# Second-layer expert biases added through the tokens' gates, transfers counted by the instruction scheduler, and eight sequences routed as 4 + 4 instead of 2 + 3 + 3

## The chip, the cores and the metric

The kernel runs on one core of a Trainium2 chip. The metric is the device time of one execution in microseconds (us). Matrix products run on TensorE (PE in the profile, its weight loads PEld), elementwise work on VectorE (DVE), ScalarE (ACT) and GpSimd (POOL). SyncE (SP) issues most of the transfers, and POOL issues the ones that gather or scatter rows by an index.

## The reference

Two layers act on eight sequences of 512 tokens with 128 channels. In each layer an attention and an expert layer read the same normalized input, and both are added to it.

```python
xn = layernorm(x)
x  = x + L0_attn(xn, ...) + L0_ffn(xn, ...)     # linear attention; top-1 of 8 experts, 128 -> 128
xn = layernorm(x)
x  = x + L1_attn(xn, ...) + L1_ffn(xn, ...)     # windowed + latent attention; top-2 of 8 experts

# L1_ffn
probs  = softmax(x_flat @ gate_w.T)
topk_probs, topk_idx = top_k(probs, 2)
hidden = relu(einsum('th,ehf->tef', x_flat, w1) + b1)        # 128 -> 512
all_out = einsum('tef,efh->teh', hidden, w2) + b2            # 512 -> 128
y = sum over the two chosen experts of all_out * topk_probs
```

In layer 1 a token's output from an expert is multiplied by the token's gate, so the part that comes from `b2` is the token's two gates times the two rows of `b2`.

## The kernel before

**Stages.** `layer0(b)` runs the first layer of sequence b: norm, projections, linear attention, and eight products with the expert weights, each with the tokens scaled by a gate (`gbc`, a gate row read back from DRAM and spread over the partitions). It ends with the normalized tokens written to `x_rows[h]` and router logits kept for group h. `attention1(b)` is the second layer's attention. Its last steps are `loc` (DVE), `aT` (POOL; the tile `aT` has one buffer), the product `fp` of `aT` with `wo1`, and an addition of `fp` to the sequence's `x1`.

**Groups.** `GROUPS` splits the sequences for the second expert layer. `route(h)` needs the logits of all sequences of group h. It finds the two best experts of each token (`pick`), their gates (`gw`), and sorts tokens by expert into tiles of 128 rows; each expert's rows are rounded up to whole tiles. It ends with `token_i` and `row_i`, the indices to gather by and to scatter to. `experts1(h)` then runs over a fixed number of tiles, `_tiles(n) = (2 * n * N + E * (P - 1)) // P` for n sequences: 23, 31 and 31. For a tile it loads w1 and w2 of the tile's expert (256 KB each) and its row of b2 spread over the partitions (64 KB), all through SP with an expert number read on the chip. POOL gathers 128 rows (`xgt`), PE transposes them (`tpx`), multiplies by w1 (`hp`), ACT adds b1 and applies the relu (`ht`), PE multiplies by w2 (`yp`), DVE adds b2 (`ys`) and POOL scatters the rows to `y_rows`. `output(b)` waits for all scatters of the group, reads two rows per token back (`yg`), multiplies them by the gates and adds them to `x1`.

**Order.** No engine chooses its order while running. The stages are first written down by a `Recorder` (line 127). `_duration` (line 395) gives each instruction a planned time and a delay after which others may use its result, `PLAN` (line 1461) gives each stage a start and an end that are turned into a rank for each instruction, and `order()` (line 238) picks, again and again, the instruction that can begin first by the planned times, and of several the one with the lower rank. Engines then execute in that order: a waiting instruction holds back all that are behind it on its engine. A DMA is planned here as the issuing engine's time and a fixed delay; what other transfers are doing does not enter. `_fill` (line 349) puts products of zeros (from line 362) ahead of a PE instruction where the plan sees a pause of 0.6 us or more and the output bank allows it.

In profile rows, buffer and sequence numbers are left out of the names. Nearly all instructions carry the line of the recorder's call, L389, so rows are told apart by tile names.

Of the kernel before, what the change touches and what calls it, by code (L numbers as in the profile page):

```python
# [10 lines left out]
F32 = mybir.dt.float32  # L11
# [3 lines left out]
ALU = mybir.AluOpType  # L15
# [4 lines left out]
P = 128  # L20
B, N, C = 8, 512, 128
H, D = 16, 8
NT = N // P
# [7 lines left out]
CHUNK = N // NLAT  # L31


GROUPS = (2, 3, 3)
GROUP_OF = [(h, i) for h, n in enumerate(GROUPS) for i in range(n)]


# [79 lines left out]
class Op:  # L117
# [1 line left out]

    __slots__ = (  # L120
        "engine", "emit", "uses", "time", "delay", "rank", "after", "before", "start", "end",
        "missing", "opens", "claims", "index", "follows", "shape", "last", "room",
    )


class Recorder:
# [6 lines left out]
    AHEAD, TURN = 60.0, 0.15  # L133

    PAUSE, FILL = 0.6, 0.8
    filled = 0
    ENGINES = {"tensor": "PE", "vector": "DVE", "scalar": "ACT", "gpsimd": "POOL", "sync": "SP"}

# [18 lines left out]
        yield  # L157
        self.group, self.share = None, 1.0

    def add(self, engine, emit, writes, reads, time, delay, shape=None):  # L160
        uses = [(a, True) for a in writes] + [(a, False) for a in reads]
        time *= self.share
        if engine == "PE" and self.ops and self.ops[-1].engine == "PE":

            op = self.ops[-1]
            same = op.uses[0][0].tensor.name == writes[0].tensor.name
            if self.group == len(self.ops) - 1 or (self.group is None and same):
                op.emit.append(emit)
                op.uses += uses
                op.time += time + (self.TURN if shape != op.last and self.group is None else 0.0)  # L170
                op.last = shape
                return
        op = Op()
        op.engine, op.emit, op.time, op.delay = engine, [emit], time, delay
        op.shape = op.last = shape
        op.index, op.follows = len(self.ops), ()
        op.uses = uses
        self.ops.append(op)
# [59 lines left out]
    def order(self):  # L238
# [24 lines left out]
        by_rank = sorted(self.ops, key=lambda op: (op.rank, op.index))  # L263
        oldest = 0
        free = dict.fromkeys(("PE", "DVE", "ACT", "POOL", "SP"), 0.0)
        shape = None
        ready = {e: [] for e in free}
        for op in self.ops:
# [5 lines left out]
        while len(out) < len(self.ops):  # L274
# [45 lines left out]
            op.room = at - max([free[e]] + [promised[t.name] for t in op.opens])  # L320
            op.start, op.end = at, at + turn + op.time
            free[e] = op.end
            for t in uses.get(op.index, ()):
                left[t.name] -= 1
                holders[t.name] = max(holders.get(t.name, 0.0), op.end + op.delay)
                if not left[t.name]:
                    slots[t.tag].append(holders[t.name])
            for other in op.before:
                lag = op.delay
                if other.engine == e and lag < 1.0:  # L330
                    lag = 0.0 if e == "PE" else 0.05
                other.start = max(other.start, op.end + lag)
                other.missing -= 1
                if not other.missing:
                    ready[other.engine].append(other)
# [33 lines left out]
class _Engine:  # L369
# [3 lines left out]
    def __getattr__(self, method):  # L373
        r, name = self._r, self._name
        call = getattr(getattr(r.nc, name), method)

        def record(*args, **kwargs):
            aps = [a for a in (*args, *kwargs.values()) if isinstance(a, bass.AP)]
            aps += [
                a.ap for a in (*args, *kwargs.values()) if isinstance(a, bass.IndirectOffsetOnAxis)  # L380
            ]
            time, delay = _duration(name, method, aps)
            shape = None
            if name == "tensor":
                rows = aps[1].shape[0]
                cols = int(np.prod(list(aps[1].shape)[1:])) if method == "matmul" else P
                shape = (rows, 32 * ((cols + 31) // 32))
            r.add(
                r.ENGINES[name], lambda: call(*args, **kwargs), aps[:1], aps[1:], time, delay, shape  # L389
            )  # L390

        return record


def _duration(engine, method, aps):


    def free(ap):
        return int(np.prod(list(ap.shape)[1:]))

    out = free(aps[0])
    if "dma" in method:
        size = 4e-6 * int(np.prod(list(aps[0].shape)))
        return (1.25, 2.4) if engine == "gpsimd" else (0.5, 2.0 + 5.0 * size)
    if engine == "tensor":
        if method == "transpose":
            return 0.13, 0.2
        if "16" in str(aps[2].tensor.dtype):
            return max(0.0006 * free(aps[2]), 0.04), 0.2
        return 2 * max(0.00094 * free(aps[2]), 0.064 + 0.00047 * free(aps[1])), 0.2  # L410
    n = max([out] + [free(a) for a in aps[1:2]])
    if engine == "scalar":
        if method == "copy":
            return (0.18 if aps[0].shape[0] == 32 else 0.08) + 0.00084 * n, 0.16
        return 0.26 + 0.0011 * n if len(aps) == 4 else 0.17 + 0.00095 * n, 0.16
    if engine == "gpsimd":
        if method == "memset":
            return 0.08 + 0.0005 * n, 0.08
        if n < 8:
            return 1.05, 0.08  # L420
        alike = int(np.prod([c for step, c in list(aps[2].ap)[1:] if step]))
        return 0.05 + (0.002 if alike <= 16 else 0.0024) * n, 0.08
    if method == "reciprocal":
        return 0.09 + 0.0062 * n, 0.12
    sbuf = all("PSUM" not in str(a.space) for a in aps)
    fast = sbuf and method in ("tensor_scalar", "tensor_scalar_mul", "tensor_scalar_add", "tensor_copy", "memset")
    both = sbuf and n < 1024 and len(aps) > 2 and free(aps[2]) > 1
    return (
        0.095 + (0.28 if len(aps) == 4 and (n == P or n < 8) else 0.0)
        + (0.0009 if fast else 0.0016 if both else 0.00102) * n,  # L430
        0.12,
    )
# [3 lines left out]
def two_layers_kernel(  # L436
# [67 lines left out]
    load(wsb[:, w_first:], wpack[:, w_first:])  # L504
    we_sb = const.tile([P, E, C], F32, name="we_sb")
    load(we_sb, expert_w, nc.scalar)

    ro_sb = const.tile([P, C], F32, name="ro_sb")
    for half in (slice(0, LC), slice(LC, P)):
# [204 lines left out]
    for h, n in enumerate(GROUPS):  # L714
# [1 line left out]
        rows = 2 * max(GROUPS) * N + _tiles(n) * P  # L716
        y_rows.append(tc.nc.dram_tensor(f"y_rows_{h}", [rows, C], F32, kind="Internal").ap())
        logits.append(keep.tile([P, n * NT, E], F32, tag=f"logits{h}", name=f"logits_{h}", bufs=1))
    places = {}


    OTHER = {
# [200 lines left out]
    def attention1(b):  # L923
# [216 lines left out]
        nc.vector.scalar_tensor_tensor(loc, gsb[:, 0, :], 1.0, pv, ALU.add, ALU.mult)  # L1140
        nc.gpsimd.tensor_tensor(aT, aT, loc, ALU.add)
        yield
        fp = bank("fp" + nm)
        for t in range(NT):
            ts = slice(t * P, (t + 1) * P)
            mm(fp[:, ts], aT[:, ts], wo1)
        xf = x1.rearrange("p t c -> p (t c)")
        nc.vector.tensor_add(xf, xf, fp)
        late[b] = x1
# [2 lines left out]
    def route(h):  # L1152
# [17 lines left out]
        nc.vector.tensor_tensor(gw[:, 1], mx2, mx, ALU.subtract)  # L1170
        nc.scalar.activation(gw[:, 1], gw[:, 1], AF.Exp, bias=zero)
        nc.vector.tensor_mul(gw[:, 1], gw[:, 1], rs)
        m = small.tile([P, GT, E], F32, tag="ex16", name="m" + nm, bufs=1)
        nc.vector.tensor_add(m, pick[:, 0], pick[:, 1])
        mf = m.rearrange("p t e -> p (t e)")
# [133 lines left out]
    def experts1(h):  # L1309
# [6 lines left out]
        def fetch(j):  # L1316
# [12 lines left out]
                fetch.last = nc.ops[-1]  # L1329
            first = work.tile([P, FF], F32, tag="w1", name=f"w1{nm}_{j}", bufs=3)  # L1330
            second = work.tile([P, NFC, C], F32, tag="w2", name=f"w2{nm}_{j}", bufs=4)
            third = work.tile([P, C], F32, tag="b2", name=f"b2{nm}_{j}", bufs=4)

            def load_first():
                e = bass.ds(numbers[j // QUAD][j % QUAD], 1)
# [3 lines left out]
                e = bass.ds(numbers[j // QUAD][j % QUAD], 1)  # L1339
                tc.nc.sync.dma_start(second, w2[e].rearrange("e (k p) c -> p (e k) c", p=P))  # L1340

            def load_third():
                e = bass.ds(numbers[j // QUAD][j % QUAD], 1)
                tc.nc.sync.dma_start(third, experts_b[e, 1].to_broadcast([P, C]))

            for move, to in ((load_first, first), (load_second, second), (load_third, third)):
                nc.add("SP", move, [to], [], 0.55, 3.3)
                nc.ops[-1].follows = (fetch.last,)
            ws[j] = first, second, third

        def gather(q):
            js = range(q * QUAD, min((q + 1) * QUAD, TILES))
# [13 lines left out]
        def scatter(j, ys):  # L1366
# [5 lines left out]
                    views[j], bass.IndirectOffsetOnAxis(ap=ids, axis=0), ys, None  # L1372
                )

            nc.add("POOL", store, [], [ys, ids], 1.25, 2.4)
            scattered[h].append(nc.ops[-1])

        def turn(q):
# [18 lines left out]
        for j in range(TILES + 1):  # L1397
# [18 lines left out]
                hts[j] = ht  # L1416
                yield
            if j:
                ht, (_, w2k, b2) = hts.pop(j - 1), ws.pop(j - 1)
                yp = bank(f"yp{nm}_{j - 1}")  # L1420
                for k in range(NFC):
                    mm(
# [1 line left out]
                        start=k == 0, stop=k == NFC - 1,  # L1424
                    )
                ys = work.tile([P, C], F32, tag="ys", name=f"ys{nm}_{j - 1}", bufs=YS)
                nc.vector.tensor_add(ys, yp[:, :C], b2)
                scatter(j - 1, ys)
                yield

# [21 lines left out]
    def load_next(b):  # L1452
        xs[b] = load_x(b)
        if b == 1:
# [6 lines left out]
    PLAN = {  # L1461
        "load": ((0, 1), (46, 47), (92, 93), (138, 139), (184, 185), (230, 231), (276, 277)),
        "layer0": (
            (0, 1), (0, 10), (1, 39), (77, 134),
            (121, 154), (178, 309), (241, 418), (313, 760),
        ),
        "route": ((68, 100), (273, 384), (789, 901)),
        "attention1": (
            (33, 150), (148, 194), (204, 270), (284, 611),
            (549, 789), (924, 1084), (1023, 1271), (1198, 1498),  # L1470
        ),
        "experts1": ((68, 410), (427, 1006), (967, 1293)),
        "output": (
            (676, 701), (627, 663), (1181, 1203), (995, 1107),
            (1262, 1379), (1408, 1425), (1456, 1524), (2493, 2506),
        ),
    }

# [77 lines left out]
```

## Time and profile before

| | |
|---|---|
| time, median of 3 runs (lowest to highest) | 643.65 us (640.91 to 647.41) |
| the profiled execution, own time | 641.01 us |
| its span, first to last instruction | 639.1 us |
| mean granted TensorE clock | 0.947 |
| PE busy / DVE busy / POOL busy / ACT busy | 563.8 / 476.3 / 402.7 / 343.9 us |
| moved by DMA | 91.63 MB, mean 143 GB/s |

Busy times are unions: where two instructions of one engine overlap, the overlap counts once. In a row for a group of instructions, the busy time is that of the group and the mean is the duration of one instruction. An fp32 matrix product shows as two matmul instructions, a transpose as one. So 85 tiles with four products each give 680 instructions `hp`.

### The profile page before, as it was taken

To read this page: it belongs to the slowest core of one execution; us is meant where nothing else is said; L and a number is where in the kernel's file an instruction comes from. 1 tells how busy PE (TensorE), PEld (TensorE's weight loads), DVE (VectorE), ACT (ScalarE), POOL (GpSimd) and SP (SyncE) were. 2 spreads that over 40 slices of the span, in tenths; PEclk is the share of its full clock that TensorE was granted. 3 is DMA by queue.
4 is the path that set the end of the run, shared out by engine and by line. 5 is a ranking of instruction groups with operands and counts; after the bars stand their busy time and mean duration, and the time that the engine had idled before them with its cause. 6 is when DMAs were issued, how large, how long until landed. Compare 5 with 4: busy or idle time off the path is not lost.

```text
span 639.1 us, 15660 instructions
## 1 busy us (share of the span) xinstructions
PE 563.8 (88%) x5487; PEld 465.2 (73%) x5487; DVE 476.3 (75%) x1297; ACT 343.9 (54%) x950; POOL 402.7 (63%) x422
## 2 busy tenths in 40 slices
PE   9989888798899898789999799888798988999894
PEld 3478576487777687678978679878586777888852
DVE  2797899979898899997768777878437552856594
ACT  3624639354947754475774474543744347457620
POOL 3045143788678559647668768867668586787562
PEclk8999999899999999999979899798989799899986
DMA  4044135264434246247545665677457485687222
GB/s 153 19 145 137 66 102 147 53 187 123 126 98 120 64 158 148 58 140 213 150 129 164 185 188 179 155 216 211 156 179 196 129 237 141 171 238 245 60 83 67
DMA packets 106532, 91.63 MB, mean 143 GB/s; under 512 B 8940, under 2 KB 84086, under 8 KB 106454
## 3 DMA queue, kind: packets, MB, share of 16 engines
q1 hardware_dynamic: 100582, 78.41, 42.1%
q0 software_dynamic: 5440, 11.15, 6.3%
q10 hardware_dynamic: 432, 1.07, 0.5%
q8 instruction: 44, 0.72, 0.5%
q14 instruction: 34, 0.28, 0.1%
HBM read 80.70 MB, written 9.90 MB: 142 GB/s over the span
## 4 chain that ended last, share of the span: by engine, by line
PE 37%; DVE 28%; POOL 12%; issue 9%; ACT 6%; DMA 6%; SPq 0%; POOLq 0%; DVEq 0%; ACTq 0%
PE yp L389 7%; PE hp L389 6%; PE sc L389 4%; DMA gbc<-gd 3%; POOL m L389 3%; PE rp L389 3%; DVE pw L389 3%; PE pv L389 3%; DVE xg L389 2%; POOL pw L389 2%; POOL xgt L389 2%; POOL y_rows L1371 2%; DVE m L389 2%; POOL xg L389 2%; DVE x L389 2%
## 5 line engine op out<-in xcount | busy, mean ns | idle before, releaser
L389 ACT ACTIVATE ht<-hp,bias 128x128 f32<-128x128 f32 x340 | 101.4, 373 | 51.2 <-PE hp L389 34.1
L1371 POOL DMA_INDIRECT y_rows<-ys,row_i x85 | 88.1, 1036 | 48.4 <-issue 9.8
L389 POOL DMA_INDIRECT xgt<-x_rows,token_i x85 | 87.4, 1029 | 24.8 <-issue 18.6
L389 PE MATMUL yp<-w,ht 128*128 128x128 f32 x680 | 94.6, 286 | 1.9 <-issue 1.6
L389 PEld LDWEIGHTS hp<-xt,w 128*128 128x128 f32 x680 | 86.6, 198 | 12.7 <-issue 6.7
L389 PE MATMUL hp<-xt,w 128*128 128x128 f32 x680 | 94.4, 285 | 1.2 <-DVE ys L389 0.7
L389 PEld LDWEIGHTS yp<-w,ht 128*128 128x128 f32 x680 | 86.9, 199 | 7.3 <-issue 5.3
L389 PE MATMUL rp<-we_sb,xg 128*128 128x128 f32 x512 | 67.9, 281 | 6.3 <-POOL xg L389 4.7
L389 PEld LDWEIGHTS rp<-we_sb,xg 128*128 128x128 f32 x512 | 62.2, 194 | 11.9 <-POOL xg L389 7.4
L389 POOL TENSOR_TENSOR xg<-xT,gbc 128x512 f32<-128x512 f32 x32 | 42.8, 1338 | 37.3 <-DMA gbc<-gd 25.9
L389 PE MATMUL pv<-pw,vb 128*32 128x64 f32 (+1 forms) x1088 | 37.9, 226 | 15.6 <-POOL pw L389 11.5
L389 PE MATMUL sc<-kT,qe 32*128 32x64 f32 x1024 | 45.7, 296 | 6.1 <-issue 4.8
L389 PEld LDWEIGHTS pv<-pw,vb 128*32 128x32 f32 x1088 | 33.7, 117 | 23.5 <-POOL pw L389 16.5
L389 PEld LDWEIGHTS sc<-kT,qe 32*128 32x128 f32 x1024 | 40.2, 205 | 11.9 <-issue 7.5
L389 POOL TENSOR_TENSOR pw<-pt,csb 128x512 f32<-128x512 f32 x32 | 42.5, 1328 | 3.5 <-DVE pt L389 3.3
L389 POOL TENSOR_TENSOR m<-m,amx 128x512 f32<-128x512 f32 x32 | 33.8, 1065 | 14.7 <-DVE amx L389 12.8
L389 POOL TENSOR_TENSOR m<-m,ard 128x512 f32<-128x512 f32 x32 | 34.4, 1076 | 12.7 <-DVE ard L389 3.4
L389 DVE TENSOR_TENSOR ys<-yp,b 128x128 f32<-128x128 f32 x85 | 23.5, 278 | 23.6 <-PE yp L389 19.5
L389 DVE TENSOR_TENSOR pw<-pt,csb 128x512 f32<-128x512 f32 x32 | 40.6, 1268 | 0.3
L389 POOL TENSOR_TENSOR le<-le,lrd 128x128 f32<-128x128 f32 (+3 forms) x32 | 24.0, 756 | 25.3 <-DVE lrd L389 18.3
L389 DVE COPY_PREDICATED m<-csb,sc 128x256 f32<-128x256 int32 x64 | 25.3, 435 | 19.5 <-issue 7.9
L389 ACT ACTIVATE m<-m,zero_b 128x512 f32<-128x512 f32 x32 | 23.2, 724 | 29.6 <-POOL m L389 29.6
(261 smaller groups left out, 1232.6 us busy)
## 6 DMA issues: line engine op xcount, KB each, us to landing
w<-in_w_dram SPq DMA_DIRECT2D x170, 256.0 KB
gbc<-gd SPq DMA_DIRECT2D x64, 256.0 KB
b<-in_experts_b_dram SPq DMA_DIRECT2D x85, 64.0 KB
yg<-y_rows SPq DMA_DIRECT2D x16, 256.0 KB
x<-in_x_dram SPq DMA_DIRECT2D x8, 256.0 KB
x_rows<-xn SPq DMA_DIRECT2D x8, 256.0 KB
out_dram<-x SPq DMA_DIRECT2D x8, 256.0 KB
xgt<-x_rows,token_i POOLq DMA_INDIRECT x85
```

The lines of the kernel that those rows point to most:

```text
L389: r.ENGINES[name], lambda: call(*args, **kwargs), aps[:1], aps[1:], time, delay, shape
L1371: tc.nc.gpsimd.indirect_dma_start(views[j], bass.IndirectOffsetOnAxis(ap=ids, axis=0), ys, None)
```

## The change

Three things change together, and the two tables that go with them.

- The groups are 4 and 4 sequences. `_tiles` then gives 39 and 39 tiles, 78 in place of 85.
- b2 is no longer loaded per tile and added to each tile's rows. It is loaded once, 8 rows of 128. `route` sums the two gated one-hot choices to `gates` (tokens by experts, two DVE instructions); `attention1(b)` transposes them (four PE transposes and an ACT copy, in `gate_rows`) and multiplies them with `b2_sb` into the bank `fp`, ahead of the products of `aT`. The move of `yp` out of PSUM, `ys`, becomes a copy on ACT.
- The recorder gives DMAs a `traffic`, the planned time for which they occupy the transfer engines. Transfers are queued one behind another in the plan, and a transfer's result is there no earlier than its traffic and `LANDING` allow. A few planned durations change (POOL's DMA delay, small DVE instructions).
- `PLAN` has other numbers for the two-group order.

```diff
-GROUPS = (2, 3, 3)
+GROUPS = (4, 4)
...
+    LANDING = 1.5
...
+            op.lag = op.delay
+            if op.traffic:
+                carried = max(carried, op.end) + op.traffic
+                op.lag = max(op.lag, carried + self.LANDING - op.end)
...
-                lag = op.delay
+                lag = op.lag
...
+            traffic = 0.0
+            if "dma" in method:
+
+                rate = 2.6 if len(aps[0].shape) == 2 and aps[0].shape[1] >= 512 else 3.3
+                traffic = rate * 4e-6 * int(np.prod(list(aps[0].shape)))
...
-        return (1.25, 2.4) if engine == "gpsimd" else (0.5, 2.0 + 5.0 * size)
+        return (1.25, 3.0) if engine == "gpsimd" else (0.5, 2.0 + 5.0 * size)
...
+    b2_sb = const.tile([E, C], F32, name="b2_sb")
+    load(b2_sb, experts_b[:, 1])
...
+        h, hb = GROUP_OF[b]
+        gT = gate_rows(gates1[h][:, hb * NT : (hb + 1) * NT], "1" + nm, lambda pool, sh, tag, name: (
+            work.tile(sh, F32, tag="loc", name=name, bufs=1)
+        ))
         fp = bank("fp" + nm)
-        for t in range(NT):
-            ts = slice(t * P, (t + 1) * P)
-            mm(fp[:, ts], aT[:, ts], wo1)
+        tiles = [slice(t * P, (t + 1) * P) for t in range(NT)]
+        for ts in tiles:
+            mm(fp[:, ts], gT[:, ts], b2_sb, start=ts.start == 0, stop=False)
+        for ts in tiles:
+            mm(fp[:, ts], aT[:, ts], wo1, start=False, stop=ts.stop == N)
...
+        both = small.tile(sh, F32, tag="rpw", name="gated" + nm, bufs=1)
+        nc.vector.tensor_tensor(both, pick, gw.unsqueeze(3).to_broadcast(sh), ALU.mult)
+        gates = small.tile([P, GT, E], F32, tag="gates", name="gates" + nm)
+        nc.vector.tensor_add(gates, both[:, 0], both[:, 1])
+        gates1[h] = gates
...
-            third = work.tile([P, C], F32, tag="b2", name=f"b2{nm}_{j}", bufs=4)
...
-            def load_third():
-                e = bass.ds(numbers[j // QUAD][j % QUAD], 1)
-                tc.nc.sync.dma_start(third, experts_b[e, 1].to_broadcast([P, C]))
-
-            for move, to in ((load_first, first), (load_second, second), (load_third, third)):
-                nc.add("SP", move, [to], [], 0.55, 3.3)
+            for move, to, traffic in ((load_first, first, 0.67), (load_second, second, 0.86)):
+                nc.add("SP", move, [to], [], 0.55, 3.3, traffic=traffic)
...
-                nc.vector.tensor_add(ys, yp[:, :C], b2)
+                nc.scalar.copy(ys, yp[:, :C])
...
         "layer0": (
-            (0, 1), (0, 10), (1, 39), (77, 134),
-            (121, 154), (178, 309), (241, 418), (313, 760),
+            (0, 13), (0, 24), (16, 86), (63, 165),
+            (136, 273), (251, 319), (306, 378), (334, 412),
         ),
-        "route": ((68, 100), (273, 384), (789, 901)),
+        "route": ((135, 253), (395, 497)),
         "attention1": (
-            (33, 150), (148, 194), (204, 270), (284, 611),
-            (549, 789), (924, 1084), (1023, 1271), (1198, 1498),
+            (16, 154), (125, 174), (255, 299), (325, 379),
+            (370, 528), (509, 643), (725, 946), (869, 1072),
         ),
-        "experts1": ((68, 410), (427, 1006), (967, 1293)),
+        "experts1": ((291, 469), (503, 868)),
```

## The prediction

> **What bounds the kernel now.** I read the page's busy times first, then the costliest groups, then asked the trace for where the expert tiles and the routing indices begin and end, and last for busy times in stretches cut at those points.
>
> ```profile
> PE 563.8 (88%) x5487; PEld 465.2 (73%) x5487; DVE 476.3 (75%) x1297; ACT 343.9 (54%) x950; POOL 402.7 (63%) x422
> ...
> L389 PE MATMUL yp<-w,ht 128*128 128x128 f32 x680 | 94.6, 286 | 1.9 <-issue 1.6 <-ACT ht L389 0.3
> L389 PE MATMUL hp<-xt,w 128*128 128x128 f32 x680 | 94.4, 285 | 1.2 <-DVE ys L389 0.7 <-ACT gsb L389 0.2 <-issue 0.2
> ...
> L389 DVE TENSOR_TENSOR ys<-yp,b 128x128 f32<-128x128 f32 x85 | 23.5, 278 | 23.6 <-PE yp L389 19.5 <-PE tpx L389 1.4 <-PE hp L389 1.2
> ...
> L389 PE MATMUL fp<-wo,aT 128*128 128x128 f32 x64 | 9.5, 295 | 4.7 <-POOL aT L389 4.7
> L389 PE MATMUL gp<-csb,g 128*8 128x128 f32 x32 | 5.6, 288 | 1.7 <-issue 0.8 <-ACT gsb L389 0.5 <-DVE g L389 0.4
> ```
>
> PE is the fullest engine. The mean of one `hp` is 285 ns, but 94.4 / 680 is 139 ns: products are pipelined, so I price PE work by a group's busy time over its count. A tile is 1.11 (`hp`) + 1.11 (`yp`) + 0.17 (`tpx`, 14.4 us over 85) = 2.4 us of PE.
>
> ```profile
> L389 PE MATMUL hp<-xt,w x680: 272/275/583, 130.1 to 598.7; 128*128 128x128 f32 x170
> L389 PE MATMUL yp<-w,ht x680: 270/275/582, 133.4 to 601.3; 128*128 128x128 f32 x170
> L389 DVE SCALAR_TENSOR_TENSOR row_i<-row,none x3: 182/192/192, 114.4 to 450.0; 128x31 int32<-128x31 f32 x2, 128x23 int32<-128x23 f32 x1
> ```
>
> These rows of tiles give first and last start. The first routing is done at 114.4 us, the first tile's product starts at 130.1, the last tile's at 601.3, and 37 us follow. Busy time by stretch (columns: stretch, length, then PE, PEld, DVE, ACT, POOL busy, granted PE clock, DMA share, GB/s):
>
> ```profile
> 0.00:114.00 114.00, 102.03 (x674) 71.92 (x675) 89.23 (x299) 59.24 (x142) 36.50 (x56) 0.99 0.36 110
> 114.00:130.00 16.00, 12.06 (x113) 6.72 (x112) 12.61 (x40) 6.08 (x11) 11.51 (x12) 0.80 0.15 35
> 130.00:214.00 84.00, 76.09 (x843) 64.36 (x842) 72.02 (x192) 52.65 (x137) 65.74 (x64) 1.00 0.43 126
> 214.00:330.00 116.00, 105.56 (x1037) 90.40 (x1035) 101.33 (x303) 70.96 (x194) 74.19 (x75) 0.98 0.51 143
> 330.00:480.00 150.00, 133.09 (x1383) 118.68 (x1381) 103.65 (x250) 81.03 (x245) 110.59 (x115) 0.93 0.60 176
> 480.00:601.00 121.00, 109.51 (x1175) 96.41 (x1175) 71.19 (x162) 68.82 (x212) 86.05 (x87) 0.94 0.65 183
> 601.00:640.00 39.00, 25.47 (x271) 16.68 (x270) 26.26 (x57) 5.09 (x11) 18.10 (x16) 0.77 0.25 72
> ```
>
> Three regimes. Up to 130 us there are no expert tiles and DVE sets the pace; PE's busy time there includes products of zeros. From 130 to 601 PE is about 90% busy in every stretch, whatever DVE does. The end is one attention's dependency chain with PE mostly idle or on zeros.
>
> **Work removed and added.** Removed with 7 of 85 tiles: PE 7 x 2.4 = 16.8 us, POOL 14 gathers and scatters of 1.03 us (14.4 us), ACT 28 `ht` of 0.30 us (8.4). Removed with the b2 loads: 85 `ys` additions, 23.5 us of DVE. Of transfers, 85 x 64 KB and 7 tiles' weights and rows, about 10 of 91.6 MB, and 99 issues on SP. Added: on PE 32 gate transposes (as `gp`, 5.6 us) and 64 instructions for gates times `b2_sb`. These use 8 of 128 rows, but the trace shows no discount for that: `we` from a one-row operand took 632 ns an instruction against 619 for one of 128 rows. So as `fp`, 9.5 us. PE's real work goes from 16.8 down to 15.1 up: nothing gained. ACT gains 78 copies, priced at the 268 ns of a 128x128 copy `pT` (21 us), and 8 of 0.57: +17 net on an engine 54% busy. It takes the place of DVE behind `yp`, for one-third of a microsecond either way; I put it at nothing, with ACT's idle time as cover (-3 to +5 us). DVE falls by about 21 us, but where PE or a chain is the bound that is worth little.
>
> So the gain has to come from placement, and I take the two instruction orders engine by engine. For every instruction ahead of a point I add its row's busy time over count. Such sums exceed the page's busy time, since neighbours overlap: over the whole program PE 661 against 563.8 (0.853) and DVE 546 against 476.3.
>
> **Step 1: the first tile comes later.** Ahead of the first `row_i` DVE has, before, 105 us of rows: layer 0 70, attention 14, routing and set-up 21. After, with four sequences to wait for: 113 + 66 + 36 = 215. The same sum was reached at 114.4 us, and between the first and second `row_i` (114.4 and 308 us) 205 us of rows took 193.6 us, 0.945 each. So the first routing ends at 114.4 + 110 x 0.945 = 218 us. The first tile followed 16, 24 and 28 us behind the three routings (gather, transpose, move); I take 21: **239 us** (226 with a pace of 0.87 and 16 us, 252 with 1.0 and 28).
> Until then PE has 206 us of real rows after, 110 before; times 0.853 this is 176 and 94. It loses 63 us where it lost 36: **27 us more**. The order shows a place: `fp` of sequence 0 now stands behind that sequence's gate transpose, which needs `gates`, at 174 of DVE's sum (about 180 us). PE has then only 149 us of real rows ahead of it (127 us of time). Behind it wait the rest of sequence 1's `rem_p` and all later products, on DVE the `aT` of sequence 1 (one buffer, read by this `fp`), and what follows them. 123 products of zeros stand ahead of the first tile, 69 before.
>
> Here a rule of the Trainium skill bears (TensorE: Matmul & The Clock Gate, Part 1, the HAM clock gate): a PE idle for a window of about 3.4 us falls to half clock. By the rule 27 us of pauses could cost up to 27 / 3.4 x 1.7 = 14 us more. The trace has it both ways: 0.80 in the stretch 114 to 130 with 4 us idle, 0.99 from 0 to 114 with 12 us idle and zeros in the pauses. Since the pauses are again given zeros I take 0 and keep 10 for the upper end.
>
> **Step 2: the tiles' stretch is shorter.** From first tile to last tile PE has 505 us of rows before (tiles 203, attention 195, layer 0 102, routing 5) and 384 after (186 + 135 + 60 + 3). Before it took 471.5 us where 505 x 0.853 = 431 is busy: 40 lost, 8.6%. After: 384 x 0.853 = 328, and 31 lost in proportion: 359. Transfers counted in the plan should take some of this: the chain of waits has six pieces of DMA over 1.8 us here, 5.2, 3.3, 1.9, 5.1, 5.2 and 6.2 at 137 to 565 us, 27 in all; most are gate rows of layer 0, of which only three sequences are left in this stretch. I take 8 off: **351 us**, so the last tile ends at 590. Ends: 366 at the 10.5% lost from 330 to 601 us, 335 if most of the DMA pieces go.
>
> **Step 3: the end is longer.** Before, when the last tile ends (601.6) the scores `sc` of the last attention's first half are done (597.6) and its latent part nearly; 37.5 us follow. After, the last tile is followed by the last attention's `lq`, `gj`, `lv`, `sl`, the end of sequence 6, and only then `sc`: 18.6 us of PE rows, or 16 us; DVE has 13 there. From those scores to the end the chain (four rounds of DVE, POOL, ACT, then `pv`, `fp`, outputs) took 41.5 us and is unchanged but for the gate products, which can go ahead of `aT`. Together **57 us** (50 with a better-packed chain without tiles, 60).
>
> Sum: 239 + 351 + 57 = 647 of span, and 1.9 lies around it (641.0 against 639.1): 649 against 641.0. The runs' median is 2.6 above the profiled execution. Since the steps are rounded up at least as often as down, I take 7 us of the 8 and forecast 650.5 as a median.
>
> **Rivals.**
> *The counted transfers pay (faster).* If waits on `gbc` and `w` were most of what PE lost, the new order, with 10 MB less to move, drops 20 of the 27 us, and early DVE, free of stalls for gate rows, reaches 0.90 a row: 229 + 339 + 54 = 622 of span, 626 as a median. For it: five of the chain's waits are gate rows, and an order that issues them earlier costs nothing. Against it: in the stretch waits of PE itself are put down to POOL's `pw`, `xg` and `le`, hardly to DMA (0.9 us on `w`). It decides from about 15 us of removed stalls on.
> *DVE's relief pays for the late start (no change).* DVE was 0.87 busy from 130 to 330 us and POOL and ACT wait on it there. With 21 us less of it, and tiles at half of PE's work, PE's loss in the tiles' stretch falls to 16 us: 239 + 344 + 54 = 637, 641.5 as a median. Against it: from 480 to 601 us DVE was 0.59 busy and PE lost as much.
> *Worse: the gates hold the front.* If sequence 1's attention, queued behind the first `fp`, in turn delays DVE's routing, the first tile comes at 252 and the clock falls in the pauses: 252 + 359 + 57 = 668, and 672 as a median.
> *The plan does not do what it says:* its transfer rates may be off, so that it spaces transfers which did not collide. Then the 8 us of step 2 are not gained: 658, inside the first case.
>
> **How the numbers follow.** About 1% (6.4 us) is what a measurement of this kernel can tell from no change. Forecast, slower at about 650: 0.38, its own range 644 to 664; the held front 0.10; no change 0.24; faster 0.28. The slower cases make 0.48. The range 622 to 668 takes in the faster case's time and most of the slow one's; the ends of the three steps together (226 + 335 + 50 and 252 + 366 + 60) would be wider, but do not fall together often.
>
> **What would show it.** Right: first `hp` at 230 to 250 us, first `row_i` near 218; PE busy about 0.9 from there to the last `yp` at 580 to 600; some 55 us behind it; about 180 products of zeros; DVE near 455 busy, ACT near 360. Wrong: a first `hp` ahead of 225 us, or PE over 0.94 busy in the tiles' stretch (the faster rival), or an end of under 48 us behind the last `yp`.

## The result: 5% slower, and the profile after

The changed kernel takes 678.91 us (median of 4 runs, 673.23 to 679.39) against 643.68 us before: a ratio of 1.052, 95% interval 1.045 to 1.060. Forecast were 650.5 us with a range up to 668. The direction was right and the size was not.

First the engines' busy times and three rows of groups from the page of the changed kernel:

```profile
PE 593.9 (88%) x5525; PEld 480.1 (71%) x5525; DVE 459.0 (68%) x1163; ACT 357.1 (53%) x1003; POOL 392.2 (58%) x408
...
L402 PE MATMUL hp<-xt,w 128*128 128x128 f32 x624 | 90.8, 293 | 8.0 <-DVE m L402 4.9
...
L402 PE MATMUL yp<-w,ht 128*128 128x128 f32 x624 | 89.2, 289 | 5.6 <-ACT ht L402 3.6
...
L402 POOL TENSOR_TENSOR xg<-xT,gbc 128x512 f32<-128x512 f32 x32 | 43.9, 1371 | 55.9 <-DMA gbc<-gd 39.6
```

There are 56 fewer `hp` and 56 fewer `yp` instructions, each a little longer (293 and 289 ns; 285 and 286 before). PE is busy 30 us more than before; 67 more products of zeros are in that. POOL waits longer for gate rows than before (39.6 us against 25.9; with the counted transfers alone, in e2 below, it is 40.3), so counting the transfers removed no wait there. The rows for the three tiles that cut the time into stretches:

```profile
L402 PE MATMUL hp<-xt,w x624: 272/275/582, 237.7 to 615.9; 128*128 128x128 f32 x156
L402 PE MATMUL yp<-w,ht x624: 272/275/582, 244.0 to 618.5; 128*128 128x128 f32 x156
L402 DVE SCALAR_TENSOR_TENSOR row_i<-row,none x2: 199/200/200, 215.8 to 459.5; 128x39 int32<-128x39 f32 x2
```

And the busy times in the three stretches, first of the kernel before, then of the changed one (columns as in the prediction):

```profile
0.00:130.00 130.00, 114.09 (x785) 78.64 (x786) 101.84 (x337) 65.32 (x153) 48.01 (x68) 0.96 0.34 101
130.00:602.00 472.00, 425.24 (x4441) 370.59 (x4439) 349.19 (x907) 273.46 (x786) 337.06 (x340) 0.96 0.56 160
602.00:639.00 37.00, 24.49 (x262) 15.94 (x262) 25.26 (x54) 5.09 (x11) 17.61 (x16) 0.77 0.26 76
```

```profile
0.00:238.00 238.00, 212.51 (x1717) 152.38 (x1718) 194.39 (x574) 123.41 (x291) 103.19 (x123) 0.94 0.25 77
238.00:619.00 381.00, 336.36 (x3319) 298.49 (x3318) 223.77 (x497) 216.48 (x669) 264.83 (x263) 0.93 0.52 155
619.00:677.00 58.00, 45.08 (x493) 29.26 (x491) 40.80 (x93) 17.24 (x44) 24.20 (x24) 0.85 0.25 71
```

| us | before | predicted | measured |
|---|---|---|---|
| start to first `hp` | 130 | 239 | 237.7 |
| first `hp` to end of last `yp` | 471.5 | 351 | 381.3 |
| behind the last `yp` | 37.5 | 57 | 57.8 |

The whole error of 30 us lies in the middle stretch: PE is idle there for 45 us of 381, and its granted clock is 0.93 where it was 0.96.

### The profile page after: what moved, and what is told of

It reads as the page before. It is cut to its first block, busy times and chain, and to the rows that moved or that the text cites. A ratio compares the mean times of both kernels' runs of the same rounds, so it can differ in the third digit from the quotient of the medians.

```text
span 676.8 us, 15212 instructions
## 1 busy us (share of the span) xinstructions
PE 593.9 (88%) x5525; PEld 480.1 (71%) x5525; DVE 459.0 (68%) x1163; ACT 357.1 (53%) x1003; POOL 392.2 (58%) x408
## 4 chain that ended last, share of the span: by engine, by line
PE 43%; DVE 24%; ACT 10%; POOL 9%; issue 8%; DMA 5%; another core or an unknown queue 1%; SPq 0%; POOLq 0%; DVEq 0%; ACTq 0%
PE hp L402 8%; PE yp L402 7%; PE sc L402 4%; PE rp L402 4%; DMA gbc<-gd 3%; PE rem_p L402 3%; PE kp L402 3%; DVE pw L402 3%; ACT vb L402 2%; PE pv L402 2%; POOL y_rows L1396 2%; DVE xg L402 2%; PE fp L402 2%; POOL m L402 2%; POOL xg L402 1%
## 5 line engine op out<-in xcount | busy, mean ns | idle before, releaser
L402 ACT ACTIVATE ht<-hp,bias 128x128 f32<-128x128 f32 x312 | 92.6, 373 | 60.4 <-PE hp L402 42.6
L1396 POOL DMA_INDIRECT y_rows<-ys,row_i x78 | 84.1, 1078 | 54.1 <-ACT ys L402 41.3
L402 PE MATMUL hp<-xt,w 128*128 128x128 f32 x624 | 90.8, 293 | 8.0 <-DVE m L402 4.9
L402 POOL DMA_INDIRECT xgt<-x_rows,token_i x78 | 78.8, 1010 | 32.1 <-issue 19.1
L402 PEld LDWEIGHTS hp<-xt,w 128*128 128x128 f32 x624 | 82.9, 205 | 17.4 <-issue 7.8
L402 PE MATMUL yp<-w,ht 128*128 128x128 f32 x624 | 89.2, 289 | 5.6 <-ACT ht L402 3.6
L402 PEld LDWEIGHTS yp<-w,ht 128*128 128x128 f32 x624 | 81.1, 201 | 9.9 <-ACT ht L402 4.8
L402 POOL TENSOR_TENSOR xg<-xT,gbc 128x512 f32<-128x512 f32 x32 | 43.9, 1371 | 55.9 <-DMA gbc<-gd 39.6
L402 PE MATMUL rp<-we_sb,xg 128*128 128x128 f32 x512 | 69.9, 284 | 5.9 <-DVE xg L402 3.6
L402 PE MATMUL sc<-kT,qe 32*128 32x64 f32 x1024 | 45.1, 288 | 13.9 <-issue 10.7
L402 ACT COPY vb<-v 32x128 f32<-32x128 f32 x128 | 37.8, 296 | 5.9 <-PE lq L402 4.0
L402 DVE TENSOR_TENSOR pw<-pt,csb 128x512 f32<-128x512 f32 x32 | 36.6, 1143 | 0.9 <-DVE x L402 0.2
```

The costliest lines, as they stand in the source:

```text
L1396: tc.nc.gpsimd.indirect_dma_start(views[j], bass.IndirectOffsetOnAxis(ap=ids, axis=0), ys, None)
```

## Experiments

The chips were of two kinds. On the chips of the result, of e1 to e4 and of e9 to e12 the kernel before takes about 644 us, on those of e5 to e8, of e13 to e16 and of e17 and e18 about 615 us. Only ratios and stretches on like chips are compared, except where the text says so; each ratio is to the kernel before on the same chip. Because the scheduler deals a new order whenever a planned instruction changes, some experiments keep the order: the instruction is planned as it was, and another one is issued in its place.

### Each part alone (chip with 644 us)

```diff
 e1  GROUPS, PLAN and DMA planning of before; gates, b2_sb, ys on ACT as changed
 e2  GROUPS, PLAN and biases of before; traffic, LANDING and planned durations as changed
 e3  the changed kernel with
-GROUPS = (4, 4)
+GROUPS = (2, 3, 3)      # and PLAN of before
 e4  the kernel before with
-GROUPS = (2, 3, 3)
+GROUPS = (4, 4)         # and PLAN as changed
```

> The kernel before with the bias part alone: b2 through the gates and ys as a copy on ACT; groups 2+3+3, the table PLAN and the scheduler's DMA model as before. Theory G (the groups of four with their table lose the time): 640 to 655 us, since 9.5 + 5.6 us of PE rows are added and 85 additions leave DVE. Theory Y (ys on ACT holds POOL's scatters and what is queued behind them): 660 us or more. Theory T (planning with counted transfers spaces the work badly): 640 to 655 us.

> The kernel before with the counted transfers alone (and the changed planned durations); groups, PLAN and biases as before. Theory T: slower by 15 us or more, 660 us up. Theories G and Y: within 10 us of before, 634 to 654 us.

> The changed kernel with the groups put back to 2+3+3 and the table PLAN of before. Theory G: 640 to 655 us, the loss is gone. Theory Y or T: 665 us or more, most of the 35 us stays.

> The kernel before with groups 4+4 and the changed kernel's PLAN alone; b2 loaded per tile and added on DVE, transfers not counted. Theory G: 670 us or more, nearly all of the loss, with the first hp near 238 us and the last yp near 615. Theories Y and T: 645 to 655 us, only what the later first tile costs, with the last yp near 590.

Ratios: e1 1.037 (1.028 to 1.045), e2 1.026 (1.020 to 1.032), e3 1.029 (1.022 to 1.037), e4 1.056 (1.049 to 1.064). By itself, the step to groups of four with their table gives as long a time as the whole change. Its profile has nearly the changed kernel's stretches, 247, 376 and 60 us:

```profile
L389 PE MATMUL hp<-xt,w x624: 272/275/582, 246.9 to 619.6; 128*128 128x128 f32 x156
L389 PE MATMUL yp<-w,ht x624: 269/275/582, 250.3 to 622.5; 128*128 128x128 f32 x156
```

But the other two parts cost 3 to 4% too, alone and together alike, and that doesn't add up to 1.052 with the groups. Each of these kernels, e4 too, also has a new order, which could be part of the cost.

### The same instructions in another order (chips with 615, 644 and 644 us)

```diff
 e5  before, _duration for DVE      e10  the changed kernel, the same edit
-        0.095 + (0.28 if ...
+        0.105 + (0.28 if ...
 e11 before, _duration for ACT
-    ... else 0.17 + 0.00095 * n, 0.16
+    ... else 0.18 + 0.00095 * n, 0.16
```

> The kernel before with the same instructions; only the planned base time of DVE instructions is 0.105 instead of 0.095, so that the scheduler deals another order. Theory N (the table PLAN and the planned times fit each other, and any change of what is planned costs by itself): 655 to 670 us, as much as the bias or the traffic part alone. Theory Y and T (those parts cost by what they do): 638 to 650 us.

> The kernel before with the same instructions, only the planned base time of ACT activations at 0.18 instead of 0.17. Theory N: 1.015 to 1.04 of before, as with the planned DVE time changed. Otherwise (that one was an unlucky order): 0.99 to 1.01.

> The changed kernel with the same instructions and only the planned base time of DVE instructions at 0.105 instead of 0.095, so another order. Theory N (the changed kernel's own table fits its planned times as little as a re-dealt one): within 1.5% of the changed kernel, to either side. If the changed kernel's table is as well fitted as that of before: 1.5 to 3% slower than the changed kernel.

Ratios: e5 1.019 (1.014 to 1.025), e11 1.028 (1.019 to 1.037). A planned time that is off by 0.01 us, and no other change, costs the kernel before 2 to 3% in both trials, as if its table PLAN were fitted to its own planned times. So e2 and e3 show nothing beyond what a new deal costs; e1 lies about 1% above e11, with overlapping intervals. e10 is 1.069 (1.060 to 1.079), against 1.050 (1.043 to 1.057) for the changed kernel on the same chip (e9, whose record is below): the changed kernel loses about 2% by a new deal as well. Like against like, on chips with 644 us, the changed kernel is 5% slower as it stands (e9) and 4% slower with both re-dealt (e10 over e11); e4, itself a re-dealt order, is 2.7% above e11. So the deal alone doesn't explain the result, the groups with their table account for most of it, and what the other two parts add can't be told from a deal.

> The changed kernel once more, so that it and the experiments on it are measured on one chip. By its first measurement: 1.045 to 1.060 of before. Theory Y is already weak; if ys on DVE were worth 2% this one would lie at 1.05 on the chip on which that kernel was 1.033.

### ys on ACT (order kept; chips with 615 us)

POOL waits on ACT's `ys` for 41 us in the changed kernel of the result, the longest of POOL's waits (waited for, total, times, longest):

```profile
POOL y_rows L1396 <- ACT ys L402: 41.3, 20, 4.6
POOL xg L402 <- DMA gbc<-gd: 39.6, 9, 24.3
```

```diff
 e6, e7  before: b2 loads planned but not issued, b2 left out
-                nc.vector.tensor_add(ys, yp[:, :C], b2)
+                nc.add("DVE", lambda ...: tc.nc.vector.tensor_copy(o, i), ...)   # e6
+                nc.add("DVE", lambda ...: tc.nc.scalar.copy(o, i), ...)          # e7
 e8, e18 changed kernel
-                nc.scalar.copy(ys, yp[:, :C])
+                nc.add("ACT", lambda ...: tc.nc.vector.tensor_copy(o, i), ...)
```

> The kernel before with its order kept: the 85 loads of b2 are planned but not issued, ys is a copy on DVE in the place of the addition, b2 is left out of the result. Theory N: 636 to 643 us, the loads' removal gains little and costs nothing. If the loads of b2 hold SP or the transfers: under 632 us.

> As the one with ys on DVE and the order kept, but ys is a copy on ACT at the same place of the order; b2 is left out of the result. Theory Y: 12 us or more above the one on DVE, and POOL waits on ACT ys by 30 us or more. Theory N: within 6 us of it.

> The changed kernel with its order kept, ys copied on DVE instead of ACT at the same place of the order. Theory Y: 665 us or less, since POOL's 41 us of waits on ACT ys go. Theory N, and theory G (groups of four leave too little beside the tiles): 673 to 683 us.

Ratios: e6 0.995 (0.989 to 1.000), e7 1.000 (0.996 to 1.004), e8 1.033 (1.027 to 1.039). In the order of before, ys on ACT costs some 0.6% against ys on DVE, and leaving out 85 loads of b2 is worth about 1% at most. e8 looks like a gain of 2% over the changed kernel's 1.05, but it ran on the other kind of chip. e17 and e18 are both kernels on one 615 us chip:

> The changed kernel beside its variant with ys on DVE, on one chip. Theory chip (the long stretch with tiles comes from a lower granted clock and the waits with it, not from ys or the weights): if the kernel before takes about 615 us here, ratio 1.03 to 1.04 and 345 to 357 us from first hp to last yp; if it takes about 644 us, 1.045 to 1.055 and 378 to 388 us. Theory Y: on a chip with 615 us 1.045 or more.

> The variant of the changed kernel with ys copied on DVE, order kept. Theory chip: within 1% of the changed kernel in the same call. Theory Y: 1.5% or more below it.

The changed kernel is at 1.032 (1.028 to 1.036) there, its variant with ys on DVE at 1.041 (1.036 to 1.046), so it gains nothing. POOL's wait on `ys` is about the same with either engine, first e17, then e18:

```profile
POOL y_rows L1396 <- ACT ys L402: 22.0, 14, 4.6
POOL y_rows L1396 <- DVE ys L1454: 20.0, 10, 7.7
```

So the 41 us don't come from the choice of ACT: on this chip half of them are absent with the same instructions, and moving the copy to DVE removes only 2 us more and no time.

### The gap, the weights, the gathers

```diff
 e12 changed kernel
-        "experts1": ((291, 469), (503, 868)),
+        "experts1": ((291, 540), (503, 868)),
 e13 (changed), e14 (before): order kept, weights loaded for the first tile alone
-                tc.nc.sync.dma_start(first, w1[e]...)
+                if loaded.setdefault("w1", (h, j)) != (h, j):
+                    return
+                tc.nc.sync.dma_start(w1_fix, w1[e]...)
 e15 (changed), e16 (before): order kept, no gathers
-                nc.gpsimd.indirect_dma_start(xg[:, a], None, x_rows[h], ...)
+                nc.add("POOL", once, ...)      # fills one constant tile, once
```

> The changed kernel with one number of PLAN changed: the first group's tiles are ranked 291 to 540 instead of 291 to 469, so that they last until the second group's begin, and PE has tiles from the first to the last hp. Theory gap (24 us without tiles before the second group at a granted clock of 0.86 cost what the prediction missed): 8 to 15 us under the changed kernel, ratio 1.03 to 1.04. Theory N and G without the gap: within 6 us of the changed kernel.

> The changed kernel with its order kept; w1 and w2 are loaded once and every tile uses these (one expert's weights), 154 loads of 256 KB are left out. Theory W (tiles wait for weights): the last yp 20 us or more earlier, ratio 1.02 or less. Theories POOL and balance: under 8 us gained, 1.04 to 1.05.

> The kernel before with its order kept and weights loaded once in the same way (168 loads left out, every tile uses one expert's weights). Theory W: 0 to 8 us gained, 0.99 to 1.0, since its tiles are spread. If it gains as much as the changed kernel, the transfers cost both alike and don't explain the difference.

> The changed kernel with its order kept; the 78 gathers are left out, and the tiles transpose a constant tile. Theory POOL: 15 us or more gained, ratio 1.025 or less. Theories W and balance: under 8 us.

> The kernel before with its order kept and its 85 gathers left out in the same way. Theory POOL: up to 6 us gained, 0.99 to 1.0, less than in the changed kernel. If it gains as much, gathers don't explain the difference.

e12: 1.057 (1.049 to 1.065), not under the changed kernel's 1.050. It has another deal as well, so a small gain could hide in it, but not the 8 to 15 us expected. Nor did the edit close the gap: 21 us without any `hp` are left in its profile (447.9 to 468.9), where the changed kernel has 28 (452.7 to 480.4). What the gap costs stays untested.

Weights once: e13 1.037 (1.033 to 1.040), e14 0.998 (0.995 to 1.001). The changed kernel is at 1.032 on a like chip, so neither gains. Four fifths of the changed kernel's traffic for tiles (512 of 640 KB each) are gone, and nothing is earlier: at a DMA share of 0.20 instead of the 0.59 of e17 the middle stretch of e13 still took 346 us. The gate rows are still loaded in both.

No gathers: e15 1.011 (1.007 to 1.015), e16 0.973 (0.968 to 0.979). Here both gain, 2.0% against the 1.032 and 2.7%: a gather (POOL's time to issue it, its transfer and the wait for it, which this doesn't separate) is worth something in either kernel, and it explains no difference between them. The last `yp` starts, first of e15, then of e16, are 14 us and 18 us earlier than those of e17 (573.0) and e7 (578.2):

```profile
L402 PE MATMUL yp<-w,ht x624: 273/275/421, 235.6 to 559.4; 128*128 128x128 f32 x156
```

```profile
L389 PE MATMUL yp<-w,ht x680: 272/275/421, 128.6 to 560.1; 128*128 128x128 f32 x170
```

### The same program on two chips

e17 is the changed kernel, instruction for instruction, on a chip with 615 us. Its middle stretch, and below it that of e7, which stands for the kernel before there (ratio 1.000, the same order):

```profile
226.00:574.00 348.00, 317.66 (x3324) 283.73 (x3325) 228.34 (x511) 216.47 (x671) 266.86 (x268) 0.98 0.59 170
```

```profile
124.00:579.00 455.00, 412.10 (x4441) 359.37 (x4440) 337.22 (x828) 288.64 (x871) 342.55 (x344) 0.98 0.53 155
```

347 us from first `hp` to last `yp`, where the other chip took 381: the stretch is 0.76 of that before (455), just the ratio of PE's rows in it (384 to 505). On the 644 us chip it is 381 to 471.5, 0.81. Two pieces of the stretch hold 23 of the 34 us. They are the gap between the two groups, and one 60 us later, where PE has mostly tiles and DVE is 0.17 busy. First the changed kernel on the 644 us chip, then e17, each cut at the same PE instructions (the counts agree within one):

```profile
456.28:480.41 24.13, 16.46 (x156) 12.33 (x154) 10.91 (x29) 10.65 (x30) 12.83 (x14) 0.81 0.22 64
539.40:582.56 43.16, 34.08 (x246) 28.12 (x245) 7.51 (x21) 22.28 (x71) 26.59 (x29) 0.86 0.55 159
```

```profile
433.32:447.93 14.61, 12.04 (x155) 8.70 (x154) 10.82 (x29) 10.63 (x30) 11.62 (x13) 1.00 0.34 102
506.43:536.38 29.95, 26.94 (x246) 22.16 (x244) 7.56 (x21) 21.53 (x70) 23.03 (x26) 1.00 0.76 220
```

The same work took 24.1 us on the one chip and 14.6 on the other, and 43.2 and 30.0. PE was idle for 32% and 21% of these pieces with a clock of 0.81 and 0.86 on the first chip, for 18% and 10% with 1.00 on the second.

The waits of PE show what was added. In the middle stretch on the 644 us chip 13.9 of PE's 44.3 us of listed waits are "issue", pauses in which it waited for nothing that the profile shows; without them 30.4 us are left, and e17 has 30.4 us of waits and no such pause. The largest of these rows is:

```profile
PE sc L402 <- issue: 6.3, 11, 1.1
```

Such pauses are 3.5 to 21 us of this stretch in all ten profiles from 644 us chips (6.8 in the kernel before), and in the ten from 615 us chips there is one of 0.9 us, in e5. In the gap they stand ahead of the fall of the clock, not behind it. From 469.1 us on, the products `sc`, for which the profile shows nothing left to wait for, come with pauses of up to 1.1 us; the clock is still full up to 471.4 us and half after it:

```profile
468.00:471.40 3.40, 1.43 (x41) 1.31 (x37) 0.99 (x4) 3.05 (x10) 2.52 (x3) 1.00 0.20 57
471.40:478.20 6.80, 5.07 (x31) 4.72 (x32) 0.00 (x0) 0.65 (x2) 1.27 (x2) 0.50 0.07 20
```

So there the pauses began at full clock, and the low clock came behind them. What makes PE pause on one kind of chip and not on the other is not shown.

## Why the prediction was right in part, and where it failed

**Step 1 was right.** The first routing ended at 215.8 us (218 predicted from the sum of DVE rows and a pace of 0.945), the first `hp` started at 237.7 (239).

**Step 3 was right.** 57.8 us behind the last tile, 57 predicted, and 56 to 60 in the nine other profiles with groups of four.

**Step 2 failed, in two terms.** The first is the deduction of 8 us for counted transfers. Nothing of it came, though its premise did: in the chain of waits the pieces of DMA over 1.8 us in the middle stretch fell from 27 us to 7.7 (one of gate rows, one of a gather), and PE's loss did not fall with them. I took DMA pieces in the chain of waits as time to be had. A piece in the chain says what ended last, not what would be gained without it. e13 and e14 show the same for the weights (e14 takes 0.998 of the time with half of the bytes moved), but five of the six pieces were gate rows of layer 0, and no run leaves these out. e2 is no better than a re-deal of the same instructions.

The second is the 359 us, PE's rows and its loss in proportion to before: 328 us busy and 31 lost. On the 615 us chips this held (347 of 455, where 0.76 x 455 = 346, with 30 lost). On the 644 us chips, for which it was made, PE was busy 336 us at a clock of 0.93, and idle 45 us, of which 13.9 are the pauses that wait for nothing in the profile (the stretch of before, from which the 31 us were taken, had 6.8 of them in 472 us). So the error of 30 us is the 8 of the deduction, 8 of work at a lower clock and 14 of idle time, the size of these pauses. Why the pauses and the lower clock come on these chips stays open.

**The clock rule was weighed in the wrong stretch.** The prediction set the Trainium skill's rule (TensorE: Matmul & The Clock Gate, Part 1, the HAM clock gate: a PE idle for about 3.4 us drops to half clock) against the front, where pauses are filled with zeros, and took 0 for it. There 0 was about right (0.94 up to the first `hp`, 0.96 before). In the middle stretch `_fill` puts no product of zeros in either kernel; in the changed order 123 are ahead of the first tile, 60 behind the last. The trace agrees with the rule where PE was not busy at all from 427 to 430.4 us and had half the clock (0.50) from there to 437.2. But it also fell to 0.50 at 471.4 us, and in the 3.4 us ahead of that PE was busy for 1.43 us, with no pause over 1.2 us. A rule on whole idle windows would not have priced that fall.

**Work removed and added** was right: PE's rows are even (the gate products `fp` from `b_sb` took 10.1 us and the transposes 4.8, 15.1 predicted), DVE is at 459 us (455), ACT at 357 (360), 183 products of zeros (180). The eight-row products cost as much as full ones:

```profile
L402 PE MATMUL fp<-wo,aT 128*128 128x128 f32 x64 | 10.2, 307 | 0.0
L402 PE MATMUL fp<-b_sb,gT 8*128 8x128 f32 x64 | 10.1, 301 | 1.0 <-ACT gT L402 0.5 <-issue 0.5
```

**Rivals.** Counted transfers that pay: no. DVE's relief: no, the stretch became longer than priced with DVE at 0.59. The held front gave 672, closest to the time, but not by its cause: the first tile came at 238, not 252. The plan spacing transfers needlessly: not told apart, since e2 can't be told from a re-deal.

**What stays open.** Why the chips differ wasn't tried, nor were the order-kept experiments without weights and gathers on a 644 us chip, nor one without gate rows. Whether zeros in the middle stretch would hold the clock there is not shown. The change of groups was only tested with its table.

No version of the runs beats the kernel before; e6, e14 and e16 are below it only because they leave work out.

## What to carry to other kernels

When work is regrouped, cut both kernels' time at the points where the first and last of that work can run, and sum the engines' rows ahead of, between and behind them: two of the three sums here were good to 2 us. Price the middle by the bound engine's rows and no better than in proportion; a DMA piece in the chain of waits is no saving until a run without the transfer shows it. In a kernel whose order comes from fitted tables, measure a re-deal of the same instructions first (2 to 3% here), and compare only what ran on one chip: a wait of 41 us on the one was 22 us on the other, with the same instructions.

## What the runs showed of the hardware

Chips differ by 4.8% on one program (644 against 615 us, kernel before), and the difference isn't a common factor: the changed kernel takes 678.9 and 634.7 us, 7.0%, with most of it in one stretch whose granted clock is 0.93 on the one and 0.98 on the other. In that stretch PE has 13.9 us of pauses on the slower chip in which it waits for nothing that the profile shows, and none on the faster. The clock fell to half behind 3.4 us in which PE was busy for 1.43 us. A verdict of 5.2% on one chip is 3.2% on another.
